# Layer one of a two-layer graph network: a tile's sum in two products, update in fours, row buffers refilled from their end

## The chip, the cores and the metric

The kernel runs on one core of a Trainium2 chip. The metric is the device time of one execution in microseconds (us). The kernel before took 2380.87 us, the median of five runs (2379.17 to 2383.08).

## What is computed

Two graph layers over 6250 nodes of 256 features and 106250 edges that are sorted by target node. Layer one is a sum of messages followed by a small gated network for each node; layer two is graph attention with four heads. Each is followed by a residual addition and a layer norm.

```python
# layer one
S = feat[src]
for r in range(2):                         # two relations
    msgs = where(rel == r, relu(relu(S @ W[r].T + b[r]) @ W[r].T + b[r]), msgs)
agg = segment_sum(msgs, dst, 6250)
i, f, g, o = split(agg @ W_ih.T + b_ih + b_hh, 4)
hn = sigmoid(o) * tanh(sigmoid(i) * tanh(g))
out0 = relu(relu(hn @ W1.T + b1) @ W2.T + b2) @ W3.T + b3
x = layernorm(x + out0)
# layer two
h = x @ W                                  # 4 heads of 64
e = leaky_relu(a_src[src] + a_dst[dst], 0.2)
alpha = softmax of e over the edges of one target
y = layernorm(segment_sum(h[src] * alpha, dst) + bias + x) * gamma + beta
x = layernorm(x + relu(y))
```

## The kernel before

**Tables.** The message of an edge depends on its source and its relation alone, so a first stage computes all 2 x 6250 of them and writes them to a table in HBM, `parts0`. A row has 768 bf16 numbers: the 256 numbers of the message as three bf16 parts, whose sum is the fp32 value.

**Tiles, windows, groups.** The edges are cut into 831 tiles (`EC`) of 128 edges. Seven tiles (`WT`) make a window, 119 in all (`NW`); the targets of a window are at most 64 consecutive nodes (`SLOTS`). Two windows make a group, 60 in all (`NG`), which stands for 128 rows of sums; the last group has one window. The first tile of the next window can still hold edges of the last target of this one, so a window also sums the tile after its own seven: 118 tiles are summed for two windows.

**Layer one's loop** (L1399) goes over the tiles, one step each. At step t GpSimd issues one gather (L1405, through the helper at L1050): 128 rows of `parts0` by an index for each partition. Four tiles share one buffer of a ring of ten named `G` (L1402), so a row buffer comes round after 40 tiles. Every seventh step VectorE builds the window's one-hot matrices (`oh0`, L1129): an edge's target against the 64 slots. Four steps later (`LAG`) TensorE sums the tile (`sum0`, L1376): three products of 256 columns, one for each part, with the one-hot matrix as weights, into PSUM rows of the window's half of the group (`fps0`). A tile that two windows share is summed in both.

**What follows a group's last tile.** `turn` (L1198) copies the sum to SBUF with ScalarE and transposes it into `faT`. When both groups of a pair are there, `update` (L1215) starts: six gates of two products each with the weights `WihT` (L1242) and an activation (L1250), the product of the gates (L1255, L1262), two small products (L1266, L1273), W3 (L1289), the residual and the layer norm (L1291 to L1305), a transposition (L1314) and the product with `Wx` (L1327), which gives layer two's rows. These are stored by SP to `rows1` (L1338) and, with what layer two needs of the node, to `kept` (L1347). SP also loads the rows of `x` at the start of an update (L1224). The 60 groups go in 28 pairs and four singles at the end.

**The order of the work** is written by hand. `turn` and `update` are generators; `Steps.step()` runs each up to its next `yield n`, which lets n steps of the loop go by. `slow` sets the pace, 3 for most of the run and 1 for the last groups. Each engine carries out its instructions in the order in which they were emitted. The buffers of `ring(pool, shape, type, name, n)` are used in turn, n of them, so a new use of a buffer waits for the last reader of the old one.

**Layer two** starts when all of `rows1` is written. Its loop (L1683) gathers a tile each step from `rows1` through the same line, L1050.

Of the kernel before, what the change touches and what calls it, by code (L numbers as in the profile page):

```python
# [31 lines left out]
F32 = mybir.dt.float32  # L32
# [8 lines left out]
P = 128  # L41
N = 6250
D = 256
# [943 lines left out]
def fast(  # L987
# [92 lines left out]
    def half_of(w):  # L1080
        return slice(SLOTS * (w % 2), SLOTS * (w % 2 + 1))
# [4 lines left out]

    pairs = [[g, g + 1] for g in range(0, NG - 4, 2)] + [[g] for g in range(NG - 4, NG)]

    W8 = WT + 1
    GS = 2 * WT + 1  # L1090
    iops = ctx.enter_context(tc.tile_pool(name="iops", bufs=1, space=PSUM))
# [26 lines left out]
    def ring(pool, shape, dtype, name, n):  # L1118

        of = rings.setdefault((name, id(pool)), [[], 0])  # L1120
        if len(of[0]) < n:
            of[0].append(pool.tile(shape, dtype, name=f"{name}_{len(of[0])}"))
        of[1] += 1
        return of[0][(of[1] - 1) % n]
# [17 lines left out]
    with (  # L1142
# [55 lines left out]
        def turn(g, i, ps, aT):  # L1198

            u = rows_in(g)  # L1200
            agg = ring(up, [P, D], F32, "agg", 3)
            if u.stop < P:
                nc.vector.memset(agg, 0.0)
            nc.scalar.copy(agg[u, :], ps[u, :])
            yield 2
            pt = ring(upp, [P, D + 2 * H], F32, "fpg", 5)[:, : 2 * P]
            for k in range(2):
                nc.tensor.transpose(  # L1208
                    pt[:, k * P : (k + 1) * P], agg[:, k * P : (k + 1) * P], ident
                )  # L1210
            nc.vector.tensor_copy(  # L1211
                aT[:, :, i * P : (i + 1) * P], pt.rearrange("p (k n) -> p k n", k=2)
            )

        def update(groups, aT):  # L1215
# [1 line left out]
            cols = len(groups) * P  # L1217
            ws = [w for g in groups for w in windows_of(g)]
            at_w = lows(ws[0], min(ws[-1], NW - 2) - ws[0] + 1) if ws[0] < NW - 1 else ()
            xn = ring(up, [P, 2, D], F32, "fxn", 3)  # L1220
            for i, g in enumerate(groups):
                for w in windows_of(g):
                    if w < NW - 1:
# [3 lines left out]
                    else:  # L1227
                        gather(xn[half_of(w), i, :], x, tail_x)
            yield 4
            hn = ring(up, [P, 2, 2 * P], F32, "fhn", 3)  # L1230
            cells = []
            for m in range(2):
                gate = {}
                for name, part, func in (
                    ("gi", 0, AF.Sigmoid),
                    ("gg", 2, AF.Tanh),
                    ("go", 3, AF.Sigmoid),
                ):
                    c = 2 * part + m
                    pg = ring(upp, [P, D + 2 * H], F32, "fpg", 5)[:, : 2 * P]  # L1240
                    for k in range(2):
                        nc.tensor.matmul(  # L1242
                            pg[:, :cols],
                            WihT_s[:, k, c * P : (c + 1) * P],
                            aT[:, k, :cols],
                            start=(k == 0),
                            stop=(k == 1),
                        )
                    gate[name] = ring(up, [P, 2 * P], F32, "f" + name, 6)
                    nc.scalar.activation(  # L1250
                        gate[name][:, :cols], pg[:, :cols], func, bias=bg[:, c : c + 1]
                    )
                    yield (slow + 1) // 2
                cell = gate["gg"][:, :cols]
                nc.vector.tensor_mul(cell, cell, gate["gi"][:, :cols])  # L1255
                cells.append((cell, gate["go"][:, :cols]))
# [4 lines left out]
            for m, (cell, go) in enumerate(cells):  # L1261
                nc.vector.tensor_mul(hn[:, m, :cols], cell, go)  # L1262
            yield slow
            p1 = ring(upp, [P, D + 2 * H], F32, "fpg", 5)[:, : 2 * P]
            for k in range(2):
                nc.tensor.matmul(  # L1266
                    p1[:, :cols], W1T_s[:, k, :], hn[:, k, :cols], start=(k == 0), stop=(k == 1)
                )
            z1 = ring(up, [P, 2 * P], F32, "fz1", 3)
            nc.scalar.activation(z1[:, :cols], p1[:, :cols], AF.Relu, bias=b1c)  # L1270
            yield slow
            p2 = ring(upp, [P, D + 2 * H], F32, "fpg", 5)[:, : 2 * P]
            nc.tensor.matmul(p2[:, :cols], W2T_s, z1[:, :cols], start=True, stop=True)  # L1273
            z2 = ring(up, [P, 2 * P], F32, "fz2", 3)
            nc.scalar.activation(z2[:, :cols], p2[:, :cols], AF.Relu, bias=b2c)
            for i, g in enumerate(groups):
                u = rows_in(g)
                nc.vector.tensor_add(xn[u, i, :], xn[u, i, :], b3r[u, :])
            yield slow
            mv = ring(up, [P, 2, 2], F32, "fmv", 3)  # L1280
            rstd = ring(up, [P, 2], F32, "frstd", 3)

            keep3 = ring(up, [P, 2, 3, D], F32, "keep3", 3)
            for i, g in enumerate(groups):
                u = rows_in(g)
                if u.stop < P:
                    nc.vector.memset(mv, 1.0)
                p3 = ring(upp, [P, D + 2 * H], F32, "fpg", 5)[:, : 2 * P]
                nc.tensor.matmul(p3, z2[:, i * P : (i + 1) * P], W3T_s, start=True, stop=True)  # L1289
                y = keep3[u, i, 0, :]  # L1290
                nc.vector.tensor_add(y, p3[u, :], xn[u, i, :])  # L1291
                st = ring(up, [P, nc.vector.BN_STATS_DIM], F32, "fst", 3)
                nc.vector.bn_stats(st[u, :], y)
                nc.vector.bn_aggr(mv[u, i, :], st[u, :])
                yield 1
# [5 lines left out]
            hs = []  # L1301
            for i, g in enumerate(groups):
                u = rows_in(g)
                y = keep3[u, i, 0, :]
                nc.vector.tensor_scalar(  # L1305
                    y, y, mv[u, i, 0:1], rstd[u, i : i + 1], op0=OP.subtract, op1=OP.mult
                )
            yield slow
            for i, g in enumerate(groups):
                u = rows_in(g)  # L1310
                y = keep3[u, i, 0, :]
                pt = ring(upp, [P, D + 2 * H], F32, "fpg", 5)[:, : 2 * P]
                for k in range(2):
                    nc.tensor.transpose(  # L1314
                        pt[:, k * P : k * P + u.stop], y[:, k * P : (k + 1) * P], ident[u, u]
                    )
                yT = ring(up, [P, 2, P], F32, "fyT", 3)
                nc.scalar.copy(yT[:, :, u], pt.rearrange("p (k n) -> p k n", k=2)[:, :, u])  # L1318
                hs.append(yT)
                nc.vector.tensor_add(keep3[u, i, 1, :], y, bias_r[u, :])  # L1320
                yield 1
            yield slow - 1
            for i, g in enumerate(groups):
                u = rows_in(g)
                ph = ring(upp, [P, D + 2 * H], F32, "fpg", 5)
                for k in range(2):
                    nc.tensor.matmul(  # L1327
                        ph[u, :], hs[i][:, k, u], Wx[:, k, :], start=(k == 0), stop=(k == 1)
                    )
                hr = ring(up, [P, D + 2 * H], F32, "hr", 5)  # L1330
                nc.scalar.copy(hr[u, :], ph[u, :])
                nc.scalar.copy(keep3[u, i, 2, :], ph[u, :D])

                in_order(stored, g)
                for w in windows_of(g):
# [8 lines left out]
                            in_offset=None,  # L1344
                        )
                yield 1
                nc.sync.dma_start(kept[g, u, :], keep3[u, i, :, :].rearrange("p c f -> p (c f)"))  # L1347

                nd = ring(up, [P, 2, H], F32, "nd", 3)
                left = ring(up, [P, 2, H], F32, "left", 3)  # L1350
# [22 lines left out]

            return P if t < EC - 1 else 17

        def sum0(w, t):  # L1376

            g, j = w // 2, t - WT * w
            tiles = tiles_of(w)[1]
            if g not in sums:  # L1380
                sums[g] = ring(eps, [P, D], F32, "fps0", 2)
            for c in range(3):
                nc.tensor.matmul(  # L1383
                    sums[g][half_of(w), :],
                    ohs[w][: lanes(t), j, :],
                    got[t][: lanes(t), c * D : (c + 1) * D],
                    start=(j == 0 and c == 0),
                    stop=(t == tiles[-1] and c == 2),
                )
            if t == tiles[-1] and w == windows_of(g)[-1]:  # L1390
                pair = next(p for p in pairs if g in p)
                if g == pair[0]:
                    turned[pair[0]] = ring(up, [P, 2, 2 * P], F32, "faT", 3)
                aT = turned[pair[0]]
                run.start(turn(g, pair.index(g), sums[g], aT))
                if g == pair[-1]:
                    run.start(update(pair, aT))

        for t in range(EC + LAG):  # L1399
            if t < EC:  # L1400
                if t % 4 == 0:
                    four = ring(rowsp, [P, WT * HA], F32, "G", 10)[:, : 6 * D]  # L1402
                    four = four.bitcast(BF16).rearrange("p (j f) -> p j f", j=4)
                got[t] = four[:, t % 4, :]
                gather(got[t][: lanes(t)], parts0, idx0[: lanes(t), t : t + 1])  # L1405
                if t % WT == 0:
                    w = t // WT
                    ohs[w] = ring(ep, [P, W8, SLOTS], BF16, "oh0", 3)
                    one_hot(ohs[w], w, len(tiles_of(w)[1]))
            k = t - LAG  # L1410
            if k >= 0:
                if k % WT == 0 and k:
                    sum0(k // WT - 1, k)
                sum0(k // WT, k)
            run.step()
        run.finish()

# [364 lines left out]
```

## Time and profile before

One execution was profiled: 2381.64 us as timed, 2379.7 us from its first instruction to its last, at a mean granted TensorE clock of 0.789 of full speed.

| | us | instructions |
|---|---|---|
| five runs, median | 2380.87 | |
| profiled execution, as timed | 2381.64 | |
| its span | 2379.7 | 26238 |
| GpSimd busy | 1593.5 (67%) | 1674 |
| TensorE busy, products | 1574.3 (66%) | 7496 |
| VectorE busy | 1243.6 (52%) | 3389 |
| ScalarE busy | 688.5 (29%) | 1846 |

Four parts follow each other: the table of messages up to 196 us, layer one's gathers to 1241 us, a passage of 32 us in which the last groups are updated, and layer two from 1273 us on. The share of each engine in three stretches of these:

| stretch, us | TensorE | VectorE | ScalarE | GpSimd | clock | GB/s |
|---|---|---|---|---|---|---|
| 400 to 600 | 160.49 | 63.39 | 67.40 | 151.34 | 0.87 | 197 |
| 1200 to 1300 | 57.17 | 30.57 | 36.88 | 53.47 | 0.76 | 131 |
| 1500 to 1700 | 103.59 | 147.37 | 38.05 | 152.00 | 0.70 | 152 |

A group of instructions in the profile reads: line, engine, operation, what it writes and reads by the program's names, how many; then the time that they were busy, the mean length of one in ns, and how long the engine stood idle just before them, with what ended that idle time. A row in order of time reads: start and length in us, engine, line, operation, and in brackets the idle time before it and its releaser. A busy time of TensorE is modelled and says little of how close it is to its peak.

### The profile page before, as it was taken

How to read it: one execution, taken by the hardware profiler on the slowest of the kernel's cores; microseconds unless marked ns; L12 is line 12 of the kernel's file. 1: busy time of each engine (PE TensorE's matmuls, PEld its weight loads, DVE VectorE, ACT ScalarE, POOL GpSimd, SP SyncE). 2: the span in 40 equal slices, each digit the busy share in tenths (PEclk: the TensorE clock that was granted, in tenths of full speed). 3: DMA queues.
4: the chain of work that ended last, by engine and by line, in shares of the span. 5: the costliest groups of instructions: out<-in, count | busy, mean ns of one | idle time of the engine just before them, and what ended most of it. 6: DMA issues, size and time to landing. Idle time of an engine off the chain costs nothing. (4 is left out here: it accounts for less than half of the span.)

```text
span 2379.7 us, 26238 instructions
## 1 busy us (share of the span) xinstructions
PE 1574.3 (66%) x7496; PEld 962.1 (40%) x7496; DVE 1243.6 (52%) x3389; ACT 688.5 (29%) x1846; POOL 1593.5 (67%) x1674
## 2 busy tenths in 40 slices
PE   8995787887787887888782455545545545545553
PEld 5663454554454554555451222222223223323331
DVE  6553232323323333333332677877777877877876
ACT  4761232332332332333342111221221221221122
POOL 0005777777777777777764777777777777777770
PEclk9996879888999898798995667667667667667666
DMA  4436566666666666667663555555555555555551
GB/s 154 155 139 192 159 198 201 187 195 202 189 193 201 197 184 201 189 192 211 196 183 104 139 154 155 146 154 156 144 154 159 143 154 159 147 149 159 150 148 38
DMA packets 173854, 394.57 MB, mean 166 GB/s; under 512 B 42540, under 2 KB 74563, under 8 KB 173699
## 3 DMA queue, kind: packets, MB, share of 16 engines
q0 software_dynamic: 93216, 274.11, 42.1%
q1 hardware_dynamic: 56736, 77.07, 9.4%
q10 hardware_dynamic: 23746, 41.63, 6.0%
q8 instruction: 60, 0.98, 0.2%
q14 instruction: 96, 0.78, 0.1%
HBM read 333.39 MB, written 59.30 MB: 165 GB/s over the span
## 5 line engine op out<-in xcount | busy, mean ns | idle before, releaser
L1050 POOL DMA_INDIRECT G<-parts,fidx x831 | 791.6, 953 | 446.7 <-DMA Wx<-in_Wg_dram 193.9
L1050 POOL DMA_INDIRECT G<-rows,fidx x831 | 797.5, 960 | 255.7 <-issue 244.2
L1671 PE MATMUL fps<-gw,oh 128*64 128x264 f32 (+1 forms) x1780 | 468.9, 476 | 240.3 <-DVE gw L1563 240.1
L1383 PE MATMUL fps<-G,oh 128*64 128x256 bf16 x2847 | 445.4, 304 | 223.0 <-DMA G<-parts,fidx 209.3
L1383 PEld LDWEIGHTS <-oh 128*64 128x64 bf16 x2847 | 269.9, 119 | 411.8 <-issue 384.0
L1671 PEld LDWEIGHTS fps<-gw,oh 128*64 128x64 f32 (+1 forms) x1780 | 247.3, 170 | 429.9 <-DVE gw L1563 256.8
L1563 DVE TENSOR_TENSOR gw<-G,bank 128x1792 f32<-128x1792 f32 (+1 forms) x178 | 264.8, 1487 | 193.8 <-ACT gw L1562 191.0
L1242 PE MATMUL fpg<-faT,fWihT 128*128 128x256 f32 (+1 forms) x768 | 207.5, 396 | 0.5 <-DVE faT L1211 0.5
L1510 PE MATMUL turn<-fident,e 128*120 128x128 f32 (+2 forms) x32 | 14.5, 454 | 236.2 <-ACT e L1704 236.2
L1291 DVE TENSOR_TENSOR keep<-fpg,fxn 128x256 f32<-128x256 f32 (+1 forms) x60 | 25.3, 421 | 254.4 <-PE fpg L1289 254.1
L1129 DVE TENSOR_TENSOR oh<-bank,fslot 128x512 bf16<-128x512 f32 (+1 forms) x179 | 152.7, 854 | 2.1 <-ACT bank L1541 2.1
L1242 PEld LDWEIGHTS fpg<-faT,fWihT 128*128 128x128 f32 x768 | 130.6, 196 | 42.3 <-issue 25.3
L1610 ACT ACTIVATE frs<-fmv,eps_c 128x1 f32<-128x1 f32 x120 | 35.3, 294 | 277.3 <-DVE gw L1557 146.9
L1510 PEld LDWEIGHTS turn<-fident,e 128*120 128x120 f32 (+2 forms) x32 | 5.4, 168 | 251.0 <-ACT e L1704 249.4
L1211 DVE COPY faT<-fpg 128x256 f32<-128x256 f32 x60 | 24.5, 409 | 152.9 <-PE fpg L1208 152.9
L1616 ACT ACTIVATE fy<-fy,frs 128x256 f32<-128x256 f32 x120 | 72.0, 600 | 108.0 <-DVE gw L1557 58.0
L1562 ACT COPY gw<-bank 128x28 f32<-128x28 f32 (+1 forms) x178 | 30.3, 170 | 244.2 <-DMA dB<-slots 110.1
L1255 DVE TENSOR_TENSOR fgg<-fgg,fgi 128x256 f32<-128x256 f32 (+1 forms) x64 | 26.1, 408 | 137.6 <-ACT fgg L1250 137.0
L929 PE MATMUL fph<-fxc,fWrT 128*128 128x512 f32 (+1 forms) x208 | 89.9, 581 | 0.7 <-ACT fhT L936 0.3
L943 PE MATMUL fpm<-fWrT,fhT 128*128 128x256 f32 x392 | 88.2, 380 | 0.0
L1327 PE MATMUL fpg<-Wx,fyT 128*128 128x264 f32 (+1 forms) x240 | 80.6, 465 | 0.4 <-ACT fyT L1318 0.4
L943 PEld LDWEIGHTS fpm<-fWrT,fhT 128*128 128x128 f32 x392 | 73.9, 190 | 14.8 <-issue 5.7
(176 smaller groups left out, 1964.2 us busy)
## 6 DMA issues: line engine op xcount, KB each, us to landing
kept<-keep SPq DMA_DIRECT2D x59, 384.0 KB
k<-kept ACTq DMA_DIRECT2D x59, 384.0 KB
parts<-ms SPq DMA_DIRECT2D x49, 384.0 KB
dB<-slots ACTq DMA_DIRECT2D x119, 128.0 KB
G<-parts,fidx POOLq DMA_INDIRECT x831
G<-rows,fidx POOLq DMA_INDIRECT x831
rows<-hr SPq DMA_DIRECT2D x118, 65.0 KB
fxn<-in_x_dram SPq DMA_DIRECT2D x118, 64.0 KB
```

Source lines behind the costliest of these rows:

```text
L929: nc.tensor.matmul(ph[:, :cols], WrT_s[:, r, k, m * P : (m + 1) * P], xc[:, k, :cols], start=(k == 0), stop=(k == 1),)
L943: nc.tensor.matmul(pm[:, r, :], hT[:, r, k, j * P : (j + 1) * P], WrT_s[:, r, k, :], start=(k == 0), stop=(k == 1),)
L1050: nc.gpsimd.indirect_dma_start(out=to_tile, out_offset=None, in_=table, in_offset=bass.IndirectOffsetOnAxis(ap=idx, axis=0),)
L1129: nc.vector.tensor_tensor(to[:, :nj, :], iota_s[:, None, :].to_broadcast([P, nj, SLOTS]), of[:, :, None].to_broadcast([P, nj, SLOTS]), op= ...
L1242: nc.tensor.matmul(pg[:, :cols], WihT_s[:, k, c * P : (c + 1) * P], aT[:, k, :cols], start=(k == 0), stop=(k == 1),)
L1327: nc.tensor.matmul(ph[u, :], hs[i][:, k, u], Wx[:, k, :], start=(k == 0), stop=(k == 1))
L1383: nc.tensor.matmul(sums[g][half_of(w), :], ohs[w][: lanes(t), j, :], got[t][: lanes(t), c * D : (c + 1) * D], start=(j == 0 and c == 0), s ...
L1562: nc.scalar.copy(gw[:, :, D:HA], ex[:, o : o + n, :])
L1563: nc.vector.tensor_mul(gw[:, :, :D].rearrange("p j (h f) -> p j h f", h=H), of[:, :n, :D].rearrange("p j (h f) -> p j h f", h=H), ex[:, o ...
L1610: nc.scalar.activation(r, mv[u, k, 1:2], AF.Ln, bias=eps_c[u])
L1616: nc.scalar.activation(y, y, AF.Identity, bias=m, scale=r)
L1671: nc.tensor.matmul(sums[g][to, :], ohj, gw, start=begins, stop=left[g] == 0 or j == WT - 1)
```

## The change

All of it lies in layer one's part of the function `fast`.

- `sum0` makes two products of a tile instead of three: one of 512 columns (the first two parts) and one of 256 (the third), which is added onto the first half. The sum thus lies in PSUM as two halves, and `turn` copies the upper one with ScalarE and adds the lower one with VectorE.
- The tile that a group's two windows share is summed once, with the one-hot matrices of both windows side by side (128 columns), and it is gathered and summed ahead of the group's other tiles (`order_of`). The tile that a group shares with the next group is still summed for both.
- The one-hot matrices are built for a group at once.
- `update` goes by four groups where it went by two (`quads`), up to the last eight groups, which go as two pairs and four singles. Its tiles are twice as wide; several rings have fewer buffers; PSUM tiles take a whole bank.
- In every second round of the ten row buffers, the four rows of a buffer are filled from the last to the first.

```diff
+    quads = [list(range(g, g + 4)) for g in range(0, NG - 8, 4)]
+    quads += [[g, g + 1] for g in range(NG - 8, NG - 4, 2)] + [[g] for g in range(NG - 4, NG)]
...
         def turn(g, i, ps, aT):
             u = rows_in(g)
-            agg = ring(up, [P, D], F32, "agg", 3)
+            agg = ring(up, [P, D], F32, "agg", 2)
...
-            nc.scalar.copy(agg[u, :], ps[u, :])
-            yield 2
-            pt = ring(upp, [P, D + 2 * H], F32, "fpg", 5)[:, : 2 * P]
+            nc.scalar.copy(agg[u, :], ps[u, D:])
+            yield 1
+            nc.vector.tensor_add(agg[u, :], agg[u, :], ps[u, :D])
+            yield 1
+            pt = ring(upp, [P, 4 * P], F32, "fpg", 5)[:, : 2 * P]
...
-            xn = ring(up, [P, 2, D], F32, "fxn", 3)
+            xn = ring(up, [P, 4, D], F32, "fxn", 3)
...
-            hn = ring(up, [P, 2, 2 * P], F32, "fhn", 3)
+            hn = ring(up, [P, 2, 4 * P], F32, "fhn", 2)
...
-                    gate[name] = ring(up, [P, 2 * P], F32, "f" + name, 6)
+                    gate[name] = ring(up, [P, 4 * P], F32, "f" + name, 2 if part == 0 else 4)
...
-            keep3 = ring(up, [P, 2, 3, D], F32, "keep3", 3)
+            keep3 = [ring(up, [P, 3, D], F32, "keep3", 6) for g in groups]
...
-                hr = ring(up, [P, D + 2 * H], F32, "hr", 5)
+                hr = ring(up, [P, D + 2 * H], F32, "hr", 4)
...
+        def order_of(g):
+            t0 = 2 * WT * g
+            own = range(t0, min(t0 + 2 * WT, EC))
+            mid = [t0 + WT] if len(windows_of(g)) == 2 else []
+            return mid + [t for t in own if t not in mid]
+
+        def sum0(g, t, last=False):
+            j = t - 2 * WT * g
+            full = len(windows_of(g)) == 2
+            to = slice(0, P) if full and j == WT else slice(0, SLOTS)
+            ohj = ohs[g][: lanes(t), j, :]
+            if full and j >= WT:
+                if j == WT:
+                    ohj = ohs[g][:, WT : WT + 2, :].rearrange("p j s -> p (j s)")
+                else:
+                    to, ohj = slice(SLOTS, P), ohs[g][: lanes(t), j + 1, :]
+            begins = g not in sums
+            if begins:
+                sums[g] = ring(eps, [P, 2 * D], F32, "fps0", 2)
+            part = got[t]
+            ends = last or (full and j == WT - 1)
+            nc.tensor.matmul(
+                sums[g][to, :], ohj, part[: lanes(t), : 2 * D], start=begins, stop=False
+            )
+            nc.tensor.matmul(
+                sums[g][to, :D], ohj, part[: lanes(t), 2 * D :], start=False, stop=ends
+            )
+            if last:
+                quad = next(q for q in quads if g in q)
+                if g == quad[0]:
+                    turned[g] = ring(up, [P, 2, 4 * P], F32, "faT", 2)
+                aT = turned[quad[0]]
+                run.start(turn(g, quad.index(g), sums[g], aT))
+                if g == quad[-1]:
+                    run.start(update(quad, aT))
+
+        order = [(g, t) for g in range(NG) for t in order_of(g)]
+        for n in range(EC + LAG):
+            if n < EC:
+                g, t = order[n]
+                k = n % 4
+                if k == 0:
+                    four = ring(rowsp, [P, WT * HA], F32, "G", 10)[:, : 6 * D]
+                    four = four.bitcast(BF16).rearrange("p (j f) -> p j f", j=4)
+
+                got[t] = four[:, 3 - k if n // 40 % 2 else k, :]
                 gather(got[t][: lanes(t)], parts0, idx0[: lanes(t), t : t + 1])
+                if t == order_of(g)[0]:
+                    ohs[g] = ring(ep, [P, 2 * W8, SLOTS], BF16, "oh0", 3)
+                    full = len(windows_of(g)) == 2
+                    one_hot(ohs[g], 2 * g, 2 * W8 if full else len(tiles_of(2 * g)[1]))
+            if n >= LAG:
+                g, t = order[n - LAG]
+                sum0(g, t, g == NG - 1 and t == EC - 1)
+                if g and t == 2 * WT * g:
+                    sum0(g - 1, t, True)
             run.step()
         run.finish()
```

## The prediction

> **What bounds the kernel now.** I read the groups of instructions first, then the busy time by stretches, then the sums of waits, then the order of time. Gathers are issued from one line, L1050, by GpSimd: 831 for layer one (parts into G), 831 for layer two (rows into G).
>
> ```profile
> L1050 POOL DMA_INDIRECT G<-parts,fidx x831 | 791.6, 953 | 446.7 <-DMA Wx<-in_Wg_dram 193.9
> L1050 POOL DMA_INDIRECT G<-rows,fidx x831 | 797.5, 960 | 255.7 <-issue 244.2
> ...
> 196.10:1240.86 1044.76, 791.63 (x831) 0.87 0.67 195
> 1272.78:2323.10 1050.32, 797.49 (x831) 0.68 0.55 151
> ```
>
> The last two rows are stretches: their length, and in them GpSimd's busy time in gathers, the granted clock, the DMA share and GB/s. Layer one's gathers fill 1044.8 us of the 2379.7 us span, one every 1044.76 / 831 = 1.257 us; layer two's come every 1.264 us. Idle before layer one's gathers is 446.7 less the single wait of 193.9 for the first: 252.8, or 0.304 us each. Layer two has the same: 255.7 less one gap of 2.9 at its start is 252.8 again. So a gather costs 0.953 us of work and a gap of 0.304 us that is alike in two stages with quite different waits.
>
> The sums of waits (total, times, longest) say whether anything ever holds a gather up.
>
> ```profile
> PE fps L1383 <- DMA G<-parts,fidx: 209.3, 255, 3.9
> ...
> POOL G L1050 <- PE fps L1383: 104.8, 344, 0.3
> ...
> POOL G L1050 <- DMA G<-parts,fidx: 21.3, 70, 0.3
> ```
>
> The gathers that name TensorE or an earlier gather as releaser were idle 0.3 us at the longest, and 104.8 / 344 = 0.305: it is the fixed gap, with a name on it. TensorE waits for rows (209.3 us in all), never the reverse. Layer one's body is thus 831 gathers at GpSimd's own pace, from 196.1 to 1240.9; TensorE, VectorE, ScalarE and SP run beside it. Only two things can be seen in the time: the pace of a gather, and what follows the last one, up to layer two's first gather at 1272.78.
>
> **The change part by part.** *Two products a tile, shared tile once.* Before, 2847 products of 256 columns are 831 x 3 and 118 x 3 more for the tiles that two windows share. Of these 118, the 59 inside a group are now done once. That leaves 831 + 59 = 890 visits with two products each, 1780 in all. A visit takes 445.4 / 2847 x 3 = 0.469 us, so at least 59 x 0.469 = 27.7 us of TensorE work goes, and some weight loads. The gather hides it: TensorE would wait 28 us longer for rows. On the time: 0.
>
> *Update by four groups.* 28 pairs and 4 singles become 13 fours, 2 pairs and 4 singles: 32 updates become 19, at twice the columns in the fours, which removes ScalarE table loads (1.28 us each) and repeated weights. All of it lies beside the gathers: 0, if the burst fits. A gate of a pair, two fp32 products that the trace shows as 4 of L1242, takes 1.13 us over 256 columns; for 512 I take twice that, 2.26. Six gates in 12 steps are 13.6 us, and 12 tile visits 5.6: 19.2 us of work in 12 x 1.257 = 15.1 us. TensorE falls 4 us behind and catches up, since all of its work for a four is less than its 56 steps of 70.4 us: 60 visits x 0.469 = 28.1, and for the update (L1242 190.1, L1327 71.9, L1266 48.7, L1289 45.9, L1208 25.1, L1314 24.6, L1273 21.3 in the stretch 200 to 1200, 427.6 us for about 55 groups, 7.8 each) 31.1. That is 59 us. On SP a four puts its 8 loads of x in one row where a pair put 4 (2.54 us for 4, so some 5 us): behind them wait the stores of hr and keep3, and behind those ScalarE's L1331 by the ring of four hr instead of five, which comes round after at least 4 x 4 steps, 20 us.
>
> *Row buffers from their end.* A gather at the head of a buffer now refills the row read last, 37 gathers back, whose sum stands 33 steps back in the order: 33 x 1.257 = 41 us of slack, and one wait then covers the next three gathers. Waits are free here by the 0.304 above, so their removal is worth 0, and at most, bounded by the spread of those gaps between the stages (none to 0.1 us in 831), nothing. Gained or lost order within a buffer changes no byte moved.
>
> *Turn.* ScalarE copies the upper half, VectorE adds the lower one: one more VectorE operation for each of 60 groups. Nearest row: L1291, also PSUM and SBUF into 128x256, 0.421 us; 25 us on an engine that is about 30% busy in this stage. Hidden, but for the last group:
>
> ```profile
> 1244.60 0.68 PE L1383 MATMUL fps<-G,oh 17*64 17x256 bf16 x3 [0.72 <-DMA G<-parts,fidx]
> ...
> 1246.52 1.28 ACT L1250 ACT_TABLE_LOAD   x1 [3.63 <-PE fpg L1242]
> ...
> 1248.08 0.35 ACT L1204 COPY agg<-fps 64x256 f32<-64x256 f32 x1
> ...
> 1248.48 0.20 PEld L1208 LDWEIGHTS fpg<-fident,agg 128*128 128x128 f32 x2 [0.24 <-ACT agg L1204]
> ...
> 1268.95 0.91 POOL L1340 DMA_INDIRECT rows<-hr,tail_i  x1 [27.16 <-ACT keep L1332]
> ```
>
> Rows are start, length, engine and operation, idle before. The last sum ends at 1245.3; its copy stands behind a table load and the gate of group 58; TensorE waits for the copy (0.24 idle), and everything behind the transposes on TensorE waits with them. The add goes in just there: 0.42 and a hand-over of 0.05 to 0.1 as between copy and transposes, about +0.5. One product fewer before it gives back 0.1. The bounds are 0 (59's later wait behind 58's work swallows it) and +1.0 (two engines' queues are crossed); I take +0.4.
>
> *Pace of the gather.* Its median is 0.946, its mean 0.953, its longest 1.200: 831 x 0.007 = 5.8 us of layer one is gathers lengthened by something. The order of time shows by what:
>
> ```profile
> 614.43 0.76 DVE L1262 TENSOR_TENSOR fhn<-fgg,fgo 128x256 f32<-128x256 f32 x2
> 614.54 1.13 POOL L1050 DMA_INDIRECT G<-parts,fidx  x1 [0.30 <-PE fps L1383]
> ...
> 627.24 0.94 POOL L1050 DMA_INDIRECT G<-parts,fidx  x1 [0.30 <-PE fpg L1289]
> 627.27 0.42 DVE L1291 TENSOR_TENSOR keep<-fpg,fxn 128x256 f32<-128x256 f32 x1 [10.82 <-PE fpg L1289]
> ...
> 634.31 0.76 DVE L1320 TENSOR_TENSOR keep<-keep,fbias 128x256 f32<-128x256 f32 x2
> 634.72 1.16 POOL L1050 DMA_INDIRECT G<-parts,fidx  x1 [0.30 <-PE fps L1383]
> ```
>
> Long gathers lie beside VectorE operations with both inputs in SBUF (L1262, L1320); beside one with an input in PSUM (L1291) they keep 0.94. The new add has one input in PSUM, so it should lengthen nothing. Of the former kind, L1255, L1262, L1278, L1305 and L1320 hold 23.4, 20.3, 20.2, 21.4 and 20.3 us of the stretch 200 to 1200, 105.6 in all. The wide form halves the count of L1255 and L1262; a 128x512 addition elsewhere (L957) took 0.69 against 2 x 0.42, so they shrink by about 18%, 8 us: 5.8 x 8 / 105.6 = -0.4. Bounds: all contention gone, -5.8; or the longer runs of VectorE (four L1278 or L1305 in a row, 1.7 us, or two wide L1262, 1.4) each cover a gather whole and cost the longest seen, 1.200 - 0.946 = 0.25: 3 runs x 13 fours x 0.25 = +9.8. I take -0.4, by the share of time.
>
> [...]
>
> **Sum.** 0 for TensorE, 0 for the updates, 0 for the waits, +0.4 at the turn, -0.4 of contention: 0.0 on a profiled 2379.7 us of span (2381.64 as timed, 0.8 above the median of 2380.87). I expect no change: 2381 us.
>
> **The rivals.** *Slower: contention grows.* Place: gathers beside VectorE's longer runs; price +7 to +10 us, about 2389; it decides from a mean gather of 0.960 in layer one, layer two's present value, where VectorE is far busier. For it: the runs double in length. Against: total VectorE time of that kind falls. 0.20.
>
> *Slower: TensorE falls 41 us behind and GpSimd begins to wait.* 59 us of a four's 70.4 leave room down to a granted clock of 0.87 x 59 / 70.4 = 0.73; at 0.70 throughout, a four takes 73.5 and loses 3.1, 13 times: 40 us, 2421. For it: the stretch 200 to 300 had 0.72. Against: the other stretches of the stage up to 1200 had 0.85 to 0.91. 0.07.
>
> *Faster: the contention goes.* Half as many wide operations miss the gathers: down to -5.8, 2375. For it, the shares are a matter of phase. Against: L1320, L1278 and L1305 keep their number. 0.12.
>
> *Faster: TensorE was the bound after all*, and its 27.7 us show: 2353. For it, 80% busy; against it, its 209.3 us of waiting for rows. That the change doesn't make TensorE lighter would be invisible by the same cover. 0.06.
>
> **How the numbers follow.** 0.55 is left for no change, with its own range of 2376.5 to 2385.5. The bound for the chances is 0.2%, 4.8 us, about what a measurement of this kernel tells from no change. Faster 0.12 + 0.06 = 0.18, slower 0.20 + 0.07 = 0.27. The range takes in both cases of contention and leaves out TensorE's two, 0.13, and a little of the edges: 2373 to 2391.
>
> **What would show it.** Gathers x831 with 0.304 idle and a mean of 0.950 to 0.956; no gather idle longer than 0.31 in the stage; the products down to 1780, TensorE's wait for rows up from 209; some 32 us from the end of layer one's gathers to layer two's first. I am wrong if a gather waits for TensorE by more than the gap, if the mean gather leaves 0.946 to 0.960, or if the passage between the layers moves by more than 2 us.

## The result and the profile after

| | kernel before | kernel after |
|---|---|---|
| median, us | 2380.56 (49 runs, 2376.89 to 2383.69) | 2385.05 (29 runs, 2380.72 to 2388.57) |
| ratio, 95% interval | | 1.0019 [1.0014, 1.0025] |
| profiled execution: as timed, span, clock | 2381.64, 2379.7, 0.789 | 2380.68, 2378.9, 0.777 |
| instructions | 26238 | 22572 |

The change costs 4.5 us. That is inside the 0.2% within which the forecast called it the same, and its interval is clear of 1. The profiled execution of the kernel after, at 2380.68 us, is shorter than any of the 29 runs; it shows where time moved between the stages, not the whole 4.5 us.

The gathers of the kernel after, for layer one and layer two (busy us, mean ns, then the idle time before them):

```profile
L1050 POOL DMA_INDIRECT G<-parts,fidx x831 | 795.4, 957 | 446.9 <-issue 212.3 <-DMA Wx<-in_Wg_dram 194.1 <-PE fps L1408 15.8
L1050 POOL DMA_INDIRECT G<-rows,fidx x831 | 796.1, 958 | 255.8 <-issue 245.1 <-DMA G<-rows,fidx 6.4 <-ACT fy L1641 1.2
```

Idle before layer one's gathers is 446.9 - 194.1 = 252.8, or 0.304 each, to the tenth what it was. The gathers themselves are longer: 795.4 against 791.6. Where the releaser had been TensorE for 104.8 us, it is now 15.8, and the profile calls most of the rest "issue". The gap lost its name and none of its length: the waits that the refill from the end takes away cost nothing. (Without that refill, in `n3_front` below, TensorE is named for 87.4 us again, and the gap is the same.)

The stages, for the kernel after and then for the one before: window, length, busy time of TensorE, its weight loads, VectorE, ScalarE and GpSimd with counts, clock, DMA share, GB/s.

```profile
196.34:1244.60 1048.26, 819.29 (x2855) 350.38 (x2857) 336.38 (x1078) 245.39 (x563) 795.43 (x831) 0.84 0.67 194
1244.60:1273.98 29.38, 16.66 (x94) 11.88 (x93) 12.55 (x57) 16.42 (x44) 1.83 (x2) 0.88 0.21 64
1273.98:2322.94 1048.96, 520.74 (x2362) 292.42 (x2362) 754.94 (x1887) 195.97 (x796) 796.12 (x831) 0.68 0.55 151
```

```profile
196.12:1240.56 1044.44, 828.79 (x4310) 524.60 (x4310) 324.84 (x1143) 341.45 (x753) 791.63 (x831) 0.87 0.67 195
1240.56:1272.78 32.22, 20.73 (x99) 14.81 (x97) 12.22 (x56) 16.82 (x45) 1.84 (x3) 0.72 0.19 58
1272.78:2323.11 1050.33, 525.09 (x2362) 293.95 (x2362) 756.08 (x1887) 196.46 (x796) 797.50 (x831) 0.68 0.55 151
```

Layer one's gathers take 3.8 us more, all of it GpSimd's busy time. The passage takes 2.8 us less, at a granted clock of 0.88 against 0.72, and layer two, where nothing was changed, 1.4 less, all of it in its gathers. What TensorE waits for in the kernel after (total us, times, longest):

```profile
PE fps L1405 <- DMA G<-parts,fidx: 197.7, 283, 3.7
...
PE fpg L1214 <- DVE agg L1210: 23.1, 28, 1.4
```

TensorE waits less for rows than before (209.3), but 23.1 us for the added VectorE operation of the turn. Together that is 11.5 more. Its busy time fell by 9.5 us and the stage is 3.8 longer, 13.3 in all, most of which these two waits account for.

**What lengthens a gather.** In order of time, kernel after, where a four's update meets the next one-hot matrices:

```profile
367.33 1.28 DVE L1268 TENSOR_TENSOR fhn<-fgg,fgo 128x512 f32<-128x512 f32 x2
368.19 1.25 POOL L1050 DMA_INDIRECT G<-parts,fidx  x1 [0.30 <-issue]
368.53 1.22 DVE L1133 TENSOR_TENSOR oh<-bank,fslot 128x1024 bf16<-128x1024 f32 x1
369.67 1.42 DVE L1284 TENSOR_TENSOR fxn<-fxn,fb3r 128x256 f32<-128x256 f32 x4
369.73 1.17 POOL L1050 DMA_INDIRECT G<-parts,fidx  x1 [0.30 <-issue]
371.21 0.95 POOL L1050 DMA_INDIRECT G<-parts,fidx  x1 [0.30 <-issue]
```

An undisturbed gather takes 0.946, the median in both kernels. The one at 368.19 takes 1.245, 0.30 more; VectorE's second wide product (both inputs in SBUF) ends at 368.61, which is 0.42 after the gather's start. The one at 369.73 takes 0.22 more, and the first of L1284's four additions ends 0.35 after its start. So what such a gather takes over 0.946 is the time from its start to the operation's end, less 0.13: 0.42 - 0.13 = 0.29, 0.35 - 0.13 = 0.22. It behaves as if it stood still from some 0.13 us after its start until the operation ends. The one-hot operation (one input in PSUM, 1.22 us) holds nobody. This gave the theory: **the price of a VectorE operation with two SBUF inputs is the chance that a gather's start falls in it, times what is left of it then, so it should go with the square of its length**, not with VectorE's busy time. The wide L1261 and L1268 are 0.69 us long where the narrow ones were 0.42. Behind the wide one-hot operation L1284's four additions come close to a gather's start, and this is a second cause.

A count over ten profiles (before, after and the eight runs below that are not on the slower chip) bears the theory out and makes it sharper. An operation counts as running if it began before the gather started and then had over 0.16 us to go. 738 gathers started while an operation with two SBUF inputs was running: 727 were held, 690 of them by what the sum above gives to within 0.01 us, the other 37 for longer. The 11 that were not held started within 0.05 us after the operation. When the operation began up to 0.13 us after the gather, with no other running, none of 90 was held. So the operation has to run already when the gather starts. Where one of the two inputs was in PSUM, 2 of 748 were held, and none of 95 beside L1291's addition. Two inputs in SBUF are not the whole condition, though: L1305, which the prediction counts among such operations, has one tensor input and two columns with one number for each partition, and it held 8 of 11 gathers in the kernel before.

What each gather takes over 0.946, put down to the operation that VectorE runs 0.13 after the gather's start (us in layer one; lines of the kernel after, and the same operations in the others):

| | before | after | n4_after | n3_front | n2_pairs | n1_narrow |
|---|---|---|---|---|---|---|
| gates' products, L1261 and L1268 | 2.5 | 5.1 | 6.6 | 5.9 | 2.3 | 2.5 |
| additions L1284 | 0.1 | 2.7 | 3.3 | 2.8 | 2.6 | 5.0 |
| L1326 and L1311 | 2.6 | 1.1 | 1.0 | 0.9 | 2.5 | 0.4 |
| all gathers over 0.946 | 6.3 | 10.0 | 11.6 | 10.9 | 8.5 | 9.0 |

The last four columns are runs told of below. The sums rise by 3.7 from before to after, which is the 3.8 of the stage. The median gather is 0.946 or 0.947 in all six, so no change of the gather as such has part in it.

### The profile page after: what moved, and what is told of

Same layout as the page of the kernel before. It is cut to its first block, busy times and chain, and to the rows that moved or that the text cites. A ratio compares the mean times of both kernels' runs of the same rounds, so it can differ in the third digit from the quotient of the medians.

```text
span 2378.9 us, 22572 instructions
## 1 busy us (share of the span) xinstructions
PE 1554.6 (65%) x6038; PEld 782.6 (33%) x6039; DVE 1254.2 (53%) x3325; ACT 591.5 (25%) x1655; POOL 1595.9 (67%) x1674
## 5 line engine op out<-in xcount | busy, mean ns | idle before, releaser
L1050 POOL DMA_INDIRECT G<-parts,fidx x831 | 795.4, 957 | 446.9 <-issue 212.3
L1050 POOL DMA_INDIRECT G<-rows,fidx x831 | 796.1, 958 | 255.8 <-issue 245.1
L1696 PE MATMUL fps<-gw,oh 128*64 128x264 f32 (+1 forms) x1780 | 463.0, 471 | 241.3 <-DVE gw L1588 241.1
L1405 PE MATMUL fps<-G,oh 128*64 128x512 bf16 (+1 forms) x889 | 360.0, 449 | 201.2 <-DMA G<-parts,fidx 197.7
L1408 PE MATMUL fps<-G,oh 128*64 128x256 bf16 (+1 forms) x890 | 256.7, 311 | 12.1 <-DMA fb2c<-in_b_dram 12.1
L1210 DVE TENSOR_TENSOR agg<-agg,fps 128x256 f32<-128x256 f32 (+1 forms) x60 | 25.1, 418 | 358.8 <-ACT agg L1208 358.8
L1405 PEld LDWEIGHTS <-oh 128*64 128x64 bf16 (+1 forms) x890 | 99.9, 117 | 267.0 <-issue 216.4
L1248 PE MATMUL fpg<-faT,fWihT 128*128 128x512 f32 (+2 forms) x456 | 186.8, 535 | 0.1
L1408 PEld LDWEIGHTS <-oh 128*64 128x64 bf16 (+1 forms) x890 | 97.6, 117 | 237.0 <-issue 233.0
L1133 DVE TENSOR_TENSOR oh<-bank,fslot 128x1024 bf16<-128x1024 f32 (+1 forms) x120 | 144.1, 1201 | 2.1 <-ACT bank L1566 2.1
L1358 DVE COPY nd<-hr 128x4 f32<-128x4 f32 (+1 forms) x60 | 12.0, 201 | 207.3 <-ACT hr L1337 207.3
L1248 PEld LDWEIGHTS fpg<-faT,fWihT 128*128 128x128 f32 x456 | 77.2, 196 | 68.1 <-issue 63.8
L1333 PE MATMUL fpg<-Wx,fyT 128*128 128x264 f32 (+1 forms) x240 | 88.4, 502 | 0.4 <-ACT fyT L1324 0.4
```

The source lines that it names most:

```text
L1050: nc.gpsimd.indirect_dma_start(out=to_tile, out_offset=None, in_=table, in_offset=bass.IndirectOffsetOnAxis(ap=idx, axis=0),)
L1133: nc.vector.tensor_tensor(to[:, :nj, :], iota_s[:, None, :].to_broadcast([P, nj, SLOTS]), of[:, :, None].to_broadcast([P, nj, SLOTS]), op= ...
L1248: nc.tensor.matmul(pg[:, :cols], WihT_s[:, k, c * P : (c + 1) * P], aT[:, k, :cols], start=(k == 0), stop=(k == 1),)
L1333: nc.tensor.matmul(ph[u, :], hs[i][:, k, u], Wx[:, k, :], start=(k == 0), stop=(k == 1))
L1405: nc.tensor.matmul(sums[g][to, :], ohj, part[: lanes(t), : 2 * D], start=begins, stop=False)
L1408: nc.tensor.matmul(sums[g][to, :D], ohj, part[: lanes(t), 2 * D :], start=False, stop=ends)
```

## The experiments

The rivals of the theory were the other parts of the change: the fours as such, the refill from the end, the wider one-hot with the turn's addition; and that the 4.5 us are nothing but noise.

### Undoing one part, on another chip

`a1_narrow`: after, with the gates' products on VectorE in pieces of 256 columns.

```diff
-                nc.vector.tensor_mul(cell, cell, gate["gi"][:, :cols])
+                for c0, cn in blocks_of(cols, 2 * P):
+                    s = slice(c0, c0 + cn)
+                    nc.vector.tensor_mul(cell[:, s], cell[:, s], gate["gi"][:, s])
...
-                nc.vector.tensor_mul(hn[:, m, :cols], cell, go)
+                for c0, cn in blocks_of(cols, 2 * P):
+                    s = slice(c0, c0 + cn)
+                    nc.vector.tensor_mul(hn[:, m, s], cell[:, s], go[:, s])
```

> The kernel after, with the products of the gates (L1261, L1268) made in pieces of 256 columns, one straight behind the other. Theory: a gather that starts beside a VectorE operation with both inputs in SBUF is held until that one operation ends, so the length of a single operation counts; layer one's gathers fall from 795.4 us busy to about 792.5, and the ratio to the kernel before from 1.0019 to about 1.0006. Rival (the length of the whole run of such operations counts, or their total time): the runs are longer than before, ratio 1.0019 to 1.0030. Rival (the turn's added operation and the passage between the layers): untouched, 1.0019.

`a2_pairs`: after, with the update by pairs again.

```diff
-    quads = [list(range(g, g + 4)) for g in range(0, NG - 8, 4)]
-    quads += [[g, g + 1] for g in range(NG - 8, NG - 4, 2)] + [[g] for g in range(NG - 4, NG)]
+    quads = pairs
```

> The kernel after, with the update by pairs again; sums in two products, shared tile first, turn with the addition and row buffers from their end all stay. Theory: all of the loss is the update by fours, ratio 1.0000 within 0.0006, layer one's gathers at 791 to 793 us busy. Rival (turn, passage or the new order of the tiles): stays at 1.0019.

`a3_front`: after, with every row buffer filled from its front.

```diff
-    got[t] = four[:, 3 - k if n // 40 % 2 else k, :]
+    got[t] = four[:, k, :]
```

> The kernel after, with the row buffers filled from the front in every round. Both theories: waits of a gather are free, ratio 1.0019 as with the kernel after. If the refill from the end saved time, this is slower than the kernel after, above 1.0025; if it cost time, near 1.0010 or lower.

`a4_again`: the kernel after, unchanged.

> The kernel after again, for a second profile and as the mark for the others on this chip. Theory: ratio 1.0019, layer one's gathers near 795 us busy, held gathers beside L1261, L1268 and L1284. Rival (the passage between the layers): gathers at 792, the passage longer than 32 us.

These four fell on a chip where the kernel before took 3148.44 us: a1 3141.85, ratio 0.9983 [0.9972, 0.9994]; a2 3142.19, 0.9989 [0.9978, 1.0000]; a3 3150.49, 1.0008 [0.9999, 1.0017]; a4 3141.76, 0.9982 [0.9972, 0.9992]. The waits of a4 show why they don't answer the question:

```profile
POOL G L1050 <- DVE gw L1588: 513.8, 26, 41.1
...
DVE s L1542 <- remote: 487.8, 26, 20.8
```

There layer two's VectorE stands still for 487.8 us on something that the profile names only "remote", and GpSimd stands behind VectorE for 513.8. GpSimd's own pace doesn't set the time of that run, so what was expected of these four stays undecided by them. The gathers are held there in the same way (14.3 us over 0.946 in layer one of a4, 11.3 in a1), but that decides nothing there. What "remote" is stays open. So the four were run again, on chips like the first.

### The same parts, on chips like the first

`n4_after`, `n2_pairs`, `n3_front` and `n1_narrow` are the kernels of a4, a2, a3 and a1.

> The kernel after once more, on a chip whose kernel before takes about 2381 us if it is such a one. Theory: ratio 1.0019; in its profile layer one's gathers are 4 to 8 us longer in all than the 791.6 of the kernel before, the held ones beside L1261, L1268, L1284 and L1326. Rival (the passage between the layers): gathers near 792, passage above 34 us.

> The kernel after with the update by pairs. Theory: ratio 1.0000 within 0.0007, layer one's gathers 791 to 794 us busy. Rival (turn, order of the tiles, passage): 1.0019 as the kernel after.

> The kernel after with the row buffers filled from the front in every round, on a chip like that of the first result. Theory: the idle time before a gather is 0.304 us with any number of waits, so the refill from the end is worth nothing; ratio 1.0015 to 1.0019 as the kernel after. Rival (the refill from the end saves waits that cost time): above 1.0025.

> The kernel after with the gate products in pieces of 256 columns, on a chip like that of the first result. Theory, as the spare additions left it (mostly held to the end of the one operation, sometimes through a run of them without a break): L1261 and L1268 hold less, but the runs of four pieces can hold a gather throughout; ratio 1.0008 to 1.0018, layer one's gathers 792 to 796 us busy. If single lengths alone counted: 1.0004 to 1.0008.

The last column of the table is the busy time of layer one's 831 gathers in the run's profile, less the 791.6 of the kernel before. The rows for n4, n2, n3 and n1 come each from its own profile:

```profile
L1050 POOL DMA_INDIRECT G<-parts,fidx x831 | 796.9, 959 | 445.6 <-issue 211.0 <-DMA Wx<-in_Wg_dram 192.9 <-PE fps L1408 16.4
```

```profile
L1050 POOL DMA_INDIRECT G<-parts,fidx x831 | 793.9, 955 | 447.6 <-issue 211.4 <-DMA Wx<-in_Wg_dram 194.7 <-PE fps L1407 18.3
```

```profile
L1050 POOL DMA_INDIRECT G<-parts,fidx x831 | 796.3, 958 | 446.2 <-DMA Wx<-in_Wg_dram 193.3 <-issue 93.8 <-PE fps L1408 87.4
```

```profile
L1050 POOL DMA_INDIRECT G<-parts,fidx x831 | 794.4, 956 | 447.4 <-issue 210.5 <-DMA Wx<-in_Wg_dram 194.5 <-PE fps L1412 14.9
```

| kernel | median, us | ratio to before | gathers in layer one |
|---|---|---|---|
| after, first result | 2385.05 | 1.0019 [1.0014, 1.0025] | +3.8 |
| n4_after | 2384.63 | 1.0015 [1.0006, 1.0024] | +5.3 |
| n3_front | 2383.43 | 1.0016 [1.0007, 1.0025] | +4.7 |
| n2_pairs | 2382.49 | 1.0006 [0.9997, 1.0015] | +2.3 |
| n1_narrow | 2379.74 | 1.0001 [0.9992, 1.0010] | +2.8 |

Each number of the last column rests on one profiled execution. How well such a sum repeats can be seen in two places: `c1_psum_y`, told of below, has the layer one of the kernel before and 791.2 us where that had 791.6; and layer two, whose code is the same in the six kernels, has 796.1 to 797.7. So the column tells before from after, but hardly the kernels after from n1.

The refill from the end is worth nothing: without it the ratio and the gathers stay where they were. By the medians, narrowing the gates' products takes the loss away, though fours, one-hot and turn all stay (refill too). Its ratio of 1.0001 is below what either theory had expected of it, 1.0008 to 1.0018 and 1.0004 to 1.0008. n3 and n1 ran on one chip and differ in these products and the refill; 9 of n1's 11 runs lie below n3's median. Going back to pairs lowers the time too, but its interval reaches both 1 and the kernel after, so it alone would settle nothing; its trace has the gates' products back at 2.3 us of held gathers, and L1284, still behind the wide one-hot, at 2.6. That the loss is noise falls: it came back in n4 and n3.

The trace of n1 at the place shown above:

```profile
367.65 1.42 DVE L1272 TENSOR_TENSOR fhn<-fgg,fgo 128x256 f32<-128x256 f32 x4
368.70 1.19 POOL L1050 DMA_INDIRECT G<-parts,fidx  x1 [0.31 <-issue]
...
370.13 1.42 DVE L1288 TENSOR_TENSOR fxn<-fxn,fb3r 128x256 f32<-128x256 f32 x4
370.19 2.17 POOL L1050 DMA_INDIRECT G<-parts,fidx  x1 [0.30 <-issue]
```

The gather at 370.19 is 1.22 longer than 0.946: it is held not to the end of one addition but through all four, which end 1.36 after its start. Four such gathers are most of L1284's 5.0 us in n1, where the gates' products are back at 2.5. Only 35 of n1's gathers are over 1.00 us, against 47 (after), 53 (n4) and 32 (before). So the trace shows the cause at L1268 taken away and the one at L1284 grown, and its +2.8 is more than the median's -1.1 against the kernel before. n1's profiled run, 2382.04, is above its median by 2.3; whether its other runs lose less at L1284 can't be seen, so that part of the loss that left with the narrow products is shown by the medians alone.

### Measuring the price by itself

Three kernels add VectorE work on a spare tile to every fourth step of layer one in the kernel before.

```diff
+            if t % 4 == 0:      # b1_four256
+                for c in range(4):
+                    s = slice(c * D, (c + 1) * D)
+                    nc.vector.tensor_add(spare[:, 0, s], spare[:, 0, s], spare[:, 1, s])
...
+            if t % 4 == 0:      # b2_one1024
+                nc.vector.tensor_add(spare[:, 0, :], spare[:, 0, :], spare[:, 1, :])
...
+            if t % 4 == 0:      # b3_psum1024: one input (iota_s) in PSUM
+                s64 = spare[:, 0, :].rearrange("p (j s) -> p j s", s=SLOTS)
+                nc.vector.tensor_tensor(
+                    s64, iota_s[:, None, :].to_broadcast([P, 4 * D // SLOTS, SLOTS]), s64, op=OP.max
+                )
```

> The kernel before, and at every fourth step of layer one four additions of 256 columns on a spare tile, both inputs in SBUF, one straight behind the other (208 runs of about 1.4 us). Theory (a gather is held to the end of the one operation that runs 0.13 us after its start): 208 runs meet about 1.1 gathers each, 0.17 to 0.25 us a time: 40 to 55 us longer. Rival (held for the whole run, or in proportion to VectorE's time): as long as or longer than with one operation of 1024 columns.

> The kernel before, and at every fourth step of layer one a single addition of 1024 columns on a spare tile, both inputs in SBUF (208 of about 1.25 us): the same elements in less VectorE time. Theory: each meets a gather and holds it for half its length on average: 208 x 0.5 to 0.65 = 105 to 135 us longer, some 2.5 times the four short ones. Rival (proportion to VectorE's time, which is smaller here): no longer than the four short ones.

> The kernel before, and at every fourth step of layer one a single operation of 1024 columns on a spare tile, one input in SBUF and the other in PSUM: as long and as many as those that cost 95 us with both inputs in SBUF. Theory (the second SBUF input is what holds a gather): ratio 1.000 to 1.002, mean gather of layer one 0.950 to 0.956. Rival (any long VectorE operation holds gathers, or VectorE's load): 1.03 to 1.04.

Layer one's gathers in b1, b2 and b3, each from its own page:

```profile
L1050 POOL DMA_INDIRECT G<-parts,fidx x831 | 861.0, 1036 | 446.1 <-DMA Wx<-in_Wg_dram 193.2 <-PE fps L1385 103.3 <-issue 87.5
```

```profile
L1050 POOL DMA_INDIRECT G<-parts,fidx x831 | 887.9, 1068 | 448.1 <-DMA Wx<-in_Wg_dram 195.2 <-PE fps L1385 98.7 <-issue 91.7
```

```profile
L1050 POOL DMA_INDIRECT G<-parts,fidx x831 | 798.0, 960 | 446.9 <-DMA Wx<-in_Wg_dram 194.1 <-PE fps L1385 115.7 <-issue 72.2
```

| kernel | added op | median, us | ratio | gathers in layer one |
|---|---|---|---|---|
| b1 | four of 256 columns | 2456.13 | 1.0314 [1.0284, 1.0345] | +69.4 |
| b2 | one of 1024 columns | 2476.04 | 1.0398 [1.0377, 1.0419] | +96.3 |
| b3 | one of 1024, an input in PSUM | 2384.79 | 1.0017 [1.0007, 1.0027] | +6.4 |

The median is that of two runs for b1 (2450.10 and 2462.15) and for b2 (2477.86 and 2474.22), and of eight for b3.

b3 is the control: the same 1.2 us of VectorE at the same place, with one input in PSUM, cost 4 us where b2 cost 95. Its operation is a maximum and not an addition, but L1291, an addition with an input in PSUM, held nothing either. Two rows from each, b2 first:

```profile
612.20 1.21 DVE L1413 TENSOR_TENSOR spare<-spare 128x1024 f32<-128x1024 f32 x1
612.47 1.76 POOL L1050 DMA_INDIRECT G<-parts,fidx  x1 [0.30 <-issue]
```

```profile
602.91 1.22 DVE L1414 TENSOR_TENSOR spare<-bank,spare 128x1024 f32<-128x1024 f32 x1
603.78 0.95 POOL L1050 DMA_INDIRECT G<-parts,fidx  x1 [0.30 <-PE fps L1385]
```

In b2 the operation ends 0.94 after the gather's start, and 0.94 - 0.13 = 0.81 is just what the gather is over 0.946. In b2 all of the 165 gathers that started while the added operation was running (with over 0.16 us to go) were held; in b3 none of 171. The 6.4 us of b3 are the kernel's own operations, L1320 (4.2 us held, 2.0 before) and L1278 (3.4, 0.1 before) above all, which lie elsewhere against the gathers there; they also put its mean gather at 0.960, above the 0.950 to 0.956 expected.

That length counts, and not busy time, is right in sign: b2 has less VectorE time in its added operations (209, 254 us) than b1 (836, 294 us) and costs more. Both sizes were missed: b2's 95 us are below the 105 to 135 expected, b1's 75 above the 40 to 55. The ratio of the two, 96.3 / 69.4 = 1.4, is far from the 2.5 that I had expected, since b1 came out so much dearer: 182 of its gathers were held to the end of one operation (22 us), and 24 through a run (52 us). The worst of them:

```profile
438.36 0.41 DVE L1255 TENSOR_TENSOR fgg<-fgg,fgi 128x256 f32<-128x256 f32 x1
438.37 4.58 POOL L1050 DMA_INDIRECT G<-parts,fidx  x1 [0.30 <-issue]
438.69 1.42 DVE L1415 TENSOR_TENSOR spare<-spare 128x256 f32<-128x256 f32 x4
440.03 0.75 DVE L1320 TENSOR_TENSOR keep<-keep,fbias 128x256 f32<-128x256 f32 x2
440.70 1.42 DVE L1415 TENSOR_TENSOR spare<-spare 128x256 f32<-128x256 f32 x4
```

Operations stand back to back until 442.12, 3.75 after the gather's start; 3.75 - 0.13 = 3.62, and the gather is 3.63 over 0.946. So the theory needs a second half: a run without a pause can count as one operation. What decides whether a gather slips in between was not tried.

### An attempt at a better kernel

`c1_psum_y`: the kernel before, with layer two's sum left in PSUM, so that two more of its operations have one SBUF input.

```diff
-            nc.vector.tensor_add(y, y, ps[u, :D])
-            read.add(g)
+            q = ps[u, :D]
+            nc.vector.tensor_add(q, y, q)
             yield 1
-            nc.vector.tensor_mul(heads(y), heads(y), den[:, :, None].to_broadcast([n, H, F]))
-            nc.vector.tensor_add(y, y, k3[u, 1, :])
+            nc.vector.tensor_mul(heads(q), heads(q), den[:, :, None].to_broadcast([n, H, F]))
+            nc.vector.tensor_add(y, q, k3[u, 1, :])
+            read.add(g)
```

> The kernel before, and in layer two's finish the sum of a node (L1596) is written back to PSUM, so that L1599 and L1600 read one input from PSUM; the same arithmetic. Theory: their share of the held gathers of layer two, about 6 of 12 us, goes: ratio 0.9970 to 0.9985, a kernel faster than both. Rival (the holds only move to the next operation, or the sum's buffer comes free later and TensorE holds layer two up): 1.000 or above.

2378.95 us, ratio 0.9994 [0.9985, 1.0003]: the lowest median of all, not shown to beat the kernel before, and short of the 0.9970 to 0.9985 expected. Layer two's gathers fell only from 797.5 to 794.9. The two operations, L1599 and L1600, held gathers for 6.4 us and hold none now, but other operations hold more: L1623 (L1622 before) now holds gathers for 3.4 us where it held them for 1.3, L1527 for 2.9 where it was 2.05.

## Why the prediction was right, and where it failed

**The bound: right.** Both kernels run layer one at GpSimd's pace, with the same gap of 0.304 us, and no gather that names TensorE as its releaser was idle for longer than 0.3 us.

**Two products, shared tile once, 0: right on the time, wrong on the work.** 889 and 890 products stand in the trace after, for 1780. But the 27.7 us of TensorE work that were to go with them don't show. The tile `fps`, into which the tiles are summed, in layer one before, after and in n2 (window, length; busy time of TensorE, its weight loads, VectorE and ScalarE; clock, DMA share, GB/s):

```profile
196.12:1240.56 1044.44, 443.60 (x2838) 0.00 (x0) 0.00 (x0) 21.34 (x58) 0.87 0.67 195
```

```profile
196.34:1244.60 1048.26, 447.25 (x1773) 0.00 (x0) 24.67 (x59) 22.02 (x59) 0.84 0.67 194
```

```profile
196.98:1243.75 1046.77, 441.16 (x1774) 0.00 (x0) 24.71 (x59) 21.73 (x59) 0.88 0.66 194
```

TensorE is busy with sums for 443.6, 447.3 and 441.2 us: 890 visits in two products take as long, by this modelled time, as 949 in three. The reckoning had let a visit keep its 0.469 us; it is 447.25 / 1773 x 2 = 0.504 now. In the whole stage TensorE's busy time fell by 9.5 us, and in n2, which has these two parts without the fours, by 14.7 at the higher clock of 0.88. None of this reached the time. These two parts were not undone alone.

**Update by fours and the waits, 0: right for TensorE and the waits** (n3 for the refill). The marker that I gave, TensorE's wait for rows above 209, was wrong: it fell to 197.7, and 23.1 appeared under the turn's addition instead. In n2, by pairs and with the same addition, the wait for rows is 223.0 and that under the addition 2.3, so it is the fours that moved the wait there.

**Pace of the gather, -0.4: the step that failed.** The prediction shared 5.8 us of contention out "by the share of time" of VectorE's operations with two SBUF inputs, so that halving the count of L1255 and L1262 came out as a gain. Measured: +3.8 and +5.3 in two profiles of the kernel after, since the price goes with an operation's length and with its place beside a gather's start.

An estimate from lengths alone has the right sign. If a gather starts every 1.257 us and operations fall anywhere against it, one of length L meets a start with more than 0.13 us to go with a chance of (L - 0.13) / 1.257 and then holds it for (L - 0.13) / 2 on average: 0.033 us at 0.42 and 0.125 at 0.69. That is 112 x 0.033 = 3.7 us for the gates' products of the 28 pairs (2.5 measured) and 52 x 0.125 = 6.5 for those of the 13 fours (5.1 to 6.6 measured, those of the last groups included). L1284's operations kept their length and went from 0.1 to 2.7 by where they lie. The bound in the prediction, 0.25 as the most that a gather can lose, did not hold either: the longest gather of the kernel after is 1.439, 0.49 over 0.946.

The mechanism was the one of my rival "contention grows", at about half of its price of 7 to 10; the mean gather, 0.957 and 0.959, lies above the 0.950 to 0.956 foretold but stayed below the 0.960 from which I let that rival decide. The row that should have told me was in the prediction: a gather of 1.13 beside two L1262, whose excess is what was left of one of them.

What in a gather is held up, no run tells: b2's 165 of 165 and b3's 0 of 171 tie it to the second SBUF input, and a gather's rows name only what it reads and writes (`G<-parts,fidx`).

**The turn at the passage, +0.4: seen, and covered by something larger.** The tail of the kernel after:

```profile
1250.58 0.35 ACT L1208 COPY agg<-fps 64x256 f32<-64x256 f32 x1
...
1250.97 0.41 DVE L1210 TENSOR_TENSOR agg<-agg,fps 64x256 f32<-64x256 f32 x1 [2.38 <-ACT agg L1208]
...
1251.43 0.44 PE L1214 MATMUL fpg<-fident,agg 128*128 128x128 f32 x2 [1.38 <-DVE agg L1210]
```

From the copy's end at 1250.93 to the transposes it is 0.50 us, where it was 1248.48 - 1248.43 = 0.05; the addition is there, +0.45. But the passage as a whole fell by 2.8, beyond the 2 that I had allowed it. By the prediction's own sign of being wrong, a passage that moves by more than 2 us, this part failed. Its length goes along with the granted clock: 33.6 at 0.65 (b1), 32.2 at 0.72 (before), 32.0 at 0.73 (n2), 31.4 at 0.75 (c1), 31.2 at 0.77 (b3), 31.0 at 0.77 (n1, n3), 29.4 and 29.5 at 0.88 (after, n4); only b2, with 32.5 at 0.76, falls out. That the clock is the cause was not tested, and what sets it there is open.

**The sum.** In the profiles 3.8 - 2.8 - 1.4, and smaller differences at both ends, make the -0.8 of the spans. The 4.5 of the medians is of the size of the gathers' own 3.8 and 5.3. Whether the passage has its high clock in the longer runs too can't be seen, since only the profiled execution has records.

That "no change" held is in part luck. Of the terms, +3.8, -2.8 and -1.4 stand where -0.4, +0.4 and nothing were forecast, and they cancel in the profiled execution; in the medians the loss of 4.5 us lies just inside the bound of 4.8, and 2385.05 just inside the 2376.5 to 2385.5 given for no change.

## What to carry to other kernels

Here a stream of GpSimd gathers set the pace, and the shape of VectorE's operations was on the critical path, though VectorE was busy for only 336.4 of the 1048.3 us of layer one. In a kernel like this, keep operations with two SBUF inputs short and apart (on every fourth step, one addition of 1024 columns cost 95 us in b2, four of 256 back to back 75 in b1), or take one input from PSUM (4 us in b3; in c1, though, other operations held more instead, and no gain was shown). Making work wider on a hidden engine saved nothing here, and layer one's gathers took 3.8 and 5.3 us more in the two profiles. Price such contention by an operation's length and place against the other engine's starts, not by its share of busy time: b2's additions were busy for less than b1's, 254 against 294 us, and cost more.

## What was not expected of the hardware

- A gather can be held through a whole run of VectorE operations: by 3.63 us in b1, through eleven of them, and by 1.22 in n1, through four.
- An operation holds a gather if it runs already when the gather starts (727 of 738); one that begins up to 0.13 us later does not (0 of 90).
- The kernel before took 3148 us on one chip and 2381 on others; the profile of the kernel after on that chip has waits on "remote".
- The passage between the layers moved by 2.8 us along with the granted clock, 0.72 to 0.88, and so hid a change of half a microsecond.
